# Rows of the next image asked for one piece a band, four bands ahead of their use

## The chip, the cores and the metric

The kernel runs on one core of one Trainium2 chip. The metric is device time in microseconds (us) of one execution, from the first to the last instruction of the program with what little lies around it; several executions are taken and their median is given. The engines are named as in the profile: PE is TensorE's matmul and PEld its weight load, DVE is VectorE, ACT is ScalarE, POOL is GpSimd, SP is SyncE. A "q" behind a name (SPq) is that engine's sequencer, which issues DMAs.

## What is computed

The input is 32 images of 96 channels and 56 x 56 pixels in float32. Two layers follow each other.

```python
# layer 0: inverted bottleneck with squeeze and excitation, 576 hidden channels
h = silu(bn(conv1x1(x, fake_quant(w1))))
h = silu(bn(depthwise3x3(h, fake_quant(w2))))
s = sigmoid(se_w2 @ silu(se_w1 @ mean(h, (2, 3))))
x = x + bn(conv1x1(h * s, fake_quant(w3)))
# layer 1: two attentions, then a gated mix of a plain and a deformable 3x3 convolution
mag = abs(rfft2(x))                      # first spectrum
ca = channel_attention(mag)              # one number a channel
sa = spatial_attention(mean(x), l2(x), resized(mean(mag)))   # one number a pixel
y = x * ca * sa
aux = concat(y, coordinates, resized(mean(abs(rfft2(y)))))   # second spectrum
offset, gate = conv3x3(aux), sigmoid(conv1x1(relu(conv3x3(aux))))
z = (1 - gate) * conv3x3(y) + gate * deformable_conv(y, offset)
out = relu(batch_norm_over_all_images(z) + x)
```

## The kernel before, in words

**Streams.** `layers` (from line 942) runs three pieces of work beside each other. The *bands* of image b are the main stream: an image has seven bands of eight rows (`NBD` = 7, `RB` = 8), and a band n is offsets (`offsets`, line 644), interpolation weights (`weights_load` and `weights`, lines 681 to 696), sampling (`sample_tiles`, line 716), the deformable convolution (`deform`, line 738) and the join with the plain convolution (`combine`, line 779). Beside them go `second(b + 1)`, which is `attend` (line 437): the projection that ends layer 0, the first spectrum, the channel and spatial attention, and the second spectrum of the next image; and `first(b + 2)`, which is `hidden` (line 203): the expansion and depthwise convolution of the image after that. `pump` (line 1015) advances the two side streams in proportion to the slots of the bands. Band 5 (`turn`, line 1009) of image b is where `second(b + 1)` is drained and the side streams start anew.

**Offsets are two bands ahead.** During band n the kernel runs `find(n + 2)`, which convolves the rows of the band after next (`joint_conv`, line 619). So the last two bands of image b already read the first rows of image b + 1. A convolution of band j reads rows 8j - 1 to 8j + 8; the sampling of band j reads rows 8j - 2 to 8j + 9 (`block_channels`, line 699).

**One buffer for y.** The image y = x * ca * sa lies in a single padded tile `yp` (line 956), so rows of the next image take the place of rows of this one as these fall free. `refill(b, upto)` (line 1034) brings rows of image b in, up to a row number, in pieces of at most eight rows, if the spatial attention of that image exists (`("sa", b) in p`). For each piece `load_rows` (line 581) issues two DMAs: the rows of layer 0's output from memory, on SP's queue (line 584), and the piece's spatial attention, broadcast to 96 partitions, on GpSimd's queue (line 586) into a tile `sab` of a pool with two buffers. Four slots later (line 1041) `attend_rows` multiplies the rows in place by both attentions on VectorE (line 592). `refill` also loads the rows of the second spectrum's feature, channel 100 of `yp`, once that feature exists (`load_freq`, line 596, on SP's queue).

**When rows are asked for, before.** At the end of band j the kernel asks for the next image's rows up to 8(j + 1) - 2, which is what band j has set free, and after band 6 for all 56 (line 1150). At the beginning of band 5 it asks for rows up to 38 (line 1113), and `flush` runs every postponed step at once, the multiplications among them. The pieces that result are 8, 8 and 6 rows at the end of band 2, 8 at the ends of bands 3, 4 and 5, and 8 and 2 at the end of band 6.

**What the second spectrum needs.** `dft_mag` (line 338) takes the image in six blocks of sixteen channels, three tiles `x2` in turn. For the second spectrum each block is loaded on SP's queue (line 361), multiplied by the spatial attention on GpSimd (`weigh`, line 366), transformed on TensorE (line 386) and copied by ScalarE (line 393). The sums over channels (line 427) end each spectrum and are read by TensorE at line 430.

**Order.** Each engine runs its instructions in order. The order on SP's queue is the order of the program text (line 1354). On the other engines a scheduler, which plans with its own durations, arranges the instructions, except where an order is kept by hand (`keep_in_program_order`: the depthwise activation, the offsets' `Abs` at line 673 and the weights' product at line 695).

**Other lines that are spoken of.** L168 is the expansion's matmul and L172 its activation; L261 and L259 are the depthwise taps on VectorE, L221 their activation; L284 to L296 the squeeze and excitation; L305 loads the hidden activations `hq` back for the projection at L323 and L329; L605 and L634 are the offsets' and the plain convolution; L654 copies the offsets out and L658 stores them, L670 loads them back as `ht`, L673 and L674 make them weights, stored at L677; L688 and L689 load these as `wc` and `wr`, L695 multiplies them; L706 copies blocks for the transposes at L710, L712 copies the result; L724 samples, L728 and L735 copy and pack; L743 is the deformable convolution; L766 and L757 make the gates of two bands at a time; L782 to L785 are the join; L1049 stores z.

Of the kernel before, what the change touches and what calls it, by code (L numbers as in the profile page):

```python
# [16 lines left out]
C, H, W = 96, 56, 56  # L17
# [3 lines left out]
RB = 8  # L21
# [9 lines left out]
PD = 2  # L31
# [3 lines left out]
NBD = H // RB  # L35
# [27 lines left out]
NQB = 8  # L63
KG = 3
AHEAD = 1
READY = 1
KS = 15
TAB = HP * WP
# [512 lines left out]
def load_rows(nc, p, yp, b, x1, r0, r1):  # L581

    rows = yp[:C, PD + r0 : PD + r1, PD : PD + W]
    nc.sync.dma_start(rows, x1.rearrange("c (h w) -> c h w", h=H)[:, r0:r1])
    sab = p["q2"].tile([C, RB, W], FP, name="sab")[:, : r1 - r0]
    nc.gpsimd.dma_start(sab, p["sa", b].rearrange("o (h w) -> o h w", h=H)[:, r0:r1].to_broadcast([C, r1 - r0, W]))
    return rows, sab


def attend_rows(nc, p, b, rows, sab):  # L590

    nc.vector.scalar_tensor_tensor(rows, rows, p["ca", b], sab, ALU.mult, ALU.mult)


def load_freq(nc, p, yp, b, r0, r1):
    nc.sync.dma_start(yp[CA - 1 : CA, PD + r0 : PD + r1, PD : PD + W], p["fq", b][:, r0:r1])
# [96 lines left out]
def weights(nc, p, wc, wr):  # L693

    p["tc"].keep_in_program_order(nc.vector.tensor_tensor(wc, wc, wr, ALU.mult))  # L695
    return wc


def block_channels(nc, p, yp, j, h):

    yt = p["yt"].tile([2 * NS, NTH, C], FP, name="yt")
    yb = p["ybl"].tile([C, NTH, 2, SB, SB], FP, name="ybl")
    src = yp[:C, j * RB : j * RB + SB, h * NTH * TS : h * NTH * TS + SB]
    for s in range(2):
        blocks = bass.AP(src.tensor, src.offset + s * TS * WY, [src.ap[0], [TS, NTH], [WY, SB], [1, SB]])
        nc.gpsimd.tensor_copy(yb[:, :, s], blocks)  # L706
    for lo, hi in ((0, 4), (4, NTH)):
        pt = bank(p)
        for t in range(lo, hi):
            nc.tensor.transpose(pt[:, (t - lo) * C : (t - lo + 1) * C], yb[:, t].rearrange("c s r x -> c (s r x)"),  # L710
                                p["w"]["ident"][:C, :C])
        nc.scalar.copy(yt[:, lo:hi].rearrange("p t c -> p (t c)"), pt[:, : (hi - lo) * C])  # L712
    return yt


def sample_tiles(nc, p, yt, s, v, group):


    pts = [(bank(p), bank(p)) for _ in group]
    for (lo, hi), pt in zip(group, pts):  # L720
        for t in range(lo, hi):
            for k in range(2):
                ps = slice(k * NS, (k + 1) * NS)
                nc.tensor.matmul(pt[k][:C, (t - lo) * KP : (t - lo + 1) * KP], yt[ps, t], s[ps, t * KP : (t + 1) * KP],  # L724
                                 start=True, stop=True)
    for (lo, hi), pt in zip(group, pts):
        for k in range(2):
            nc.scalar.copy(v[:C, :, lo:hi, k].rearrange("c k t p -> c t k p"),  # L728
                           pt[k][:C, : (hi - lo) * KP].rearrange("c (t k p) -> c t k p", t=hi - lo, k=NTAP))


def pack(nc, v):

    for i in range(3):
        nc.scalar.copy(v[C:, 1 + 2 * i : 3 + 2 * i], v[i * QC : (i + 1) * QC, KA:])  # L735
# [25 lines left out]
def gates_of(nc, p, hid):  # L761

    pgs = bank(p), bank(p)
    for i, pg in enumerate(pgs):
        ps = slice(i * NS, i * NS + DMID)
        nc.tensor.matmul(pg[:C, :BW], p["w"]["dg2p"][ps], hid[ps], start=True, stop=True)  # L766
    return [gate_from(nc, p, pg) for pg in pgs]
# [174 lines left out]
def layers(tc, a, dp, x1d, zd, stats, far):  # L942
# [7 lines left out]
    B = x1d.shape[0]  # L950
    with ExitStack() as ctx:
# [8 lines left out]
                                 ("ca", 2), ("s1p", 1), ("xc", 2), ("sp", 1), ("sq", 1), ("q1", 3), ("q2", 2), ("hid", 2), ("yb", 4),  # L960
                                 ("off", 1), ("st", 2), ("ht", 1), ("wc", READY + AHEAD + 1), ("wr", AHEAD + 1), ("yt", 2), ("ybl", 1),
                                 ("vp", 2)))
# [18 lines left out]
        def flush():  # L981
            while later:
                later.pop(0)[1]()
# [27 lines left out]
        def start(b, length):  # L1011
            streams[:] = [[second(b + 1), 0, n_second, slot + 3, slot + length - 8],
                          [first(b + 2), 0, n_first, slot, slot + length]]

        def pump():
            nonlocal slot
            slot += 1
            for st in streams:
                due = st[2] * min(1.0, (slot - st[3]) / (st[4] - st[3]))
                while st[1] < due:  # L1020
                    st[1] += 1
                    next(st[0], None)
            later.sort(key=lambda e: e[0])
            while later and later[0][0] <= slot:
                later.pop(0)[1]()

        def drain():
            for st in streams:
                for _ in st[0]:
                    pass  # L1030
# [3 lines left out]
        def refill(b, upto):  # L1034

            upto = min(H, upto)
            r = filled.get(("y", b), 0)
            while ("sa", b) in p and r < upto:
                r1 = min(upto, r + RB)
                args = load_rows(nc, p, yp, b, x1d[b], r, r1)  # L1040
                later.append((slot + 4, lambda args=args: attend_rows(nc, p, b, *args)))
                r = filled["y", b] = r1
            r = filled.get(("fq", b), 0)
            if ("fq", b) in p and r < upto:
                load_freq(nc, p, yp, b, r, upto)
                filled["fq", b] = upto
# [29 lines left out]
        bands = [(b, j) for b in range(B) for j in range(NBD)]  # L1076
        hids, gates, ybs, hds, ready = [], [], [], [], []

        def find(n):
            if n % 2 == 0:  # L1080
                hids.append(p["hid"].tile([2 * NS, BW], FP, name="hid"))
            hid = hids[n // 2][n % 2 * NS : n % 2 * NS + DMID]
            return offsets(nc, p, yp, bands[n][1], top[:, n % NBD : n % NBD + 1], hid, ybs, hds)
# [11 lines left out]
        def prepare(upto):  # L1095

            nonlocal n_loads
            while n_loads < min(upto, 2 * len(hds)):
                n, m = divmod(n_loads, 2)
                loads.append(weights_load(nc, p, hds[n], m))  # L1100
                n_loads += 1

        prepare(READY + AHEAD)
        for _ in range(READY):
            ready.append(weights(nc, p, *loads.pop(0)))
        yts = [block_channels(nc, p, yp, 0, 0)]
        start(0, turn * (NTX + 2))
        for n, (b, j) in enumerate(bands):
            if j == 0:
                st = p["st"].tile([C, NBD, 6], FP, name="st")  # L1110
            if j == turn:
                drain()
                refill(b + 1, j * RB - PD)
                flush()
                start(b + 1, slots)
            more = find(n + 2) if n + 2 < len(bands) else iter(())
            next(more, None)
            for h in range(2):
                v = p["vp"].tile([128, NTAP, NTH, 2, TP], FP, name="v")
                prepare(2 * n + h + READY + AHEAD)  # L1120
                s = ready.pop(0)
                yt = yts.pop(0)
                for i, group in enumerate(GROUPS):
                    sample_tiles(nc, p, yt, s, v, group)
                    for _ in range(group[0][0], group[-1][1]):
                        next(more, None)
                        pump()
                    if i == 0:
                        for end in ends:
                            end()  # L1130
                        ends.clear()
                        if h == 1 and n + 1 < len(bands):
                            yts.append(block_channels(nc, p, yp, bands[n + 1][1], 0))
                        ready.extend(weights(nc, p, *ws) for ws in loads[:1])
                        del loads[:1]
                        if h == 0:
                            yts.append(block_channels(nc, p, yp, j, 1))
                pack(nc, v)
                if h == 0:
                    if n % 2 == 0:  # L1140
                        gates.extend(gates_of(nc, p, hids[n // 2]))
                    gate = gates.pop(0)
                ends.append(lambda n=n, h=h, v=v, gate=gate, st=st: end_half(n, h, v, gate, st))
            for _ in more:
                pass
            pump()
            pump()
            pump()
            if b + 1 < B:
                refill(b + 1, (j + 1) * RB - PD if j < NBD - 1 else H)  # L1150
            if j == NBD - 1:
                nc.vector.tensor_reduce(top[:, NBD:], top, AX.X, ALU.max)
        for end in ends:
# [349 lines left out]
```

## Time and profile before

| what | value |
|---|---|
| median of three runs | 9370.22 us (9349.59 to 9405.27) |
| the profiled execution | 9376.95 us, its span 9375.2 us |
| TensorE busy, mean granted clock | 8247.2 us (88%), 0.929 |
| VectorE busy | 7137.8 us (76%) |
| ScalarE busy | 5367.0 us (57%) |
| GpSimd busy | 2663.1 us (28%) |
| row multiplications (L592) | 255 |
| row loads (L584), attention loads (L586), feature loads (L596) | 255, 255, 100 |

How to read the lines of the profile. A group line names the source line, the engine, the operation, the tiles written and read, their shapes, how often it ran, its busy time and mean duration, and the idle time of the engine just before it with what ended that idle time ("releaser"). A line of waits names an engine and the instruction that it could not start, what ended the wait, and then the total, the count and the longest. A line of a timeline has the start (us from the span's start), the duration, the engine, the instruction, "x" with a count where neighbours are merged, and in brackets the idle time before it and its releaser; "issue" means that the profile shows nothing that was waited for. A line of windows has a stretch of time, its length, the busy time of each engine with its number of instructions, then the granted clock (1.00 is full), the share of the DMA engines' time and GB/s. A float32 matmul is two passes in the profile, so seven matmuls of the program are fourteen instructions.

### The profile page before, as it was taken

What the parts mean: (1) busy time and instruction counts of PE and PEld (TensorE: products, weight loads), DVE (VectorE), ACT (ScalarE), POOL (GpSimd) and SP (SyncE); (2) the same over time, 40 slices, a digit from 0 to 9 for tenths busy, and PEclk for the clock granted to TensorE, in tenths of its full rate; (3) what the DMA queues carried; (4) which work ended last, traced back from release to release, by engine and by line L of the source; (5) the groups of instructions that cost most, each with busy time, mean ns of one, the idle gap of its engine ahead of it and who ended that gap; (6) DMA issues with size and microseconds to landing.
All of it is one profiled execution on the core that took longest, in us unless ns stands there. A gap on an engine that the chain in (4) does not pass through costs nothing. (4 is left out here: it accounts for less than half of the span.)

```text
span 9375.2 us, 138185 instructions
## 1 busy us (share of the span) xinstructions
PE 8247.2 (88%) x52406; PEld 5235.2 (56%) x52406; DVE 7137.8 (76%) x6724; ACT 5367.0 (57%) x10486; POOL 2663.1 (28%) x2642
## 2 busy tenths in 40 slices
PE   6889999999998999899999999999999999999870
PEld 3455555565555555555555555555555555555550
DVE  7687778888777888877788888778888877887333
ACT  2355555666655566656566655556665565665453
POOL 0123233333323332332333333233223323333210
PEclk9889999999999999999999999999999999999885
DMA  2345555555555555555555555555555555555559
GB/s 89 100 138 155 156 162 158 162 149 147 156 160 158 160 162 146 145 158 158 160 159 156 151 148 161 159 160 157 156 151 148 163 161 159 160 157 140 128 172 417
DMA packets 1069507, 1486.53 MB, mean 159 GB/s; under 512 B 590438, under 2 KB 840086, under 8 KB 1056550
## 3 DMA queue, kind: packets, MB, share of 16 engines
q1 hardware_dynamic: 858747, 985.20, 38.6%
q10 hardware_dynamic: 153803, 329.80, 9.5%
q0 software_dynamic: 56288, 162.60, 6.9%
q8 instruction: 421, 6.90, 0.3%
q14 instruction: 248, 2.03, 0.1%
HBM read 1064.29 MB, written 412.65 MB: 158 GB/s over the span
## 5 line engine op out<-in xcount | busy, mean ns | idle before, releaser
L261 DVE SCALAR_TENSOR_TENSOR acch<-hp,w,acch 128x1512 f32<-128x1512 f32 (+1 forms) x2250 | 4316.7, 1919 | 35.5
L743 PE MATMUL pd<-v,c_def 128*96 128x224 f32 (+1 forms) x6272 | 1489.9, 387 | 242.9 <-ACT v L735 210.3
L605 PE MATMUL mm<-yp,c_jointW 104*128 104x448 f32 x4032 | 1671.2, 566 | 2.3 <-DMA yp<-fqd 1.8
L706 POOL COPY ybl<-yp 96x448 f32<-96x448 f32 x896 | 1131.3, 1289 | 1643.6 <-PE mm L710 1641.8
L743 PEld LDWEIGHTS pd<-v,c_def 128*96 128x96 f32 (+1 forms) x6272 | 1074.9, 178 | 553.8 <-ACT v L735 244.5
L605 PEld LDWEIGHTS mm<-yp,c_jointW 104*128 104x128 f32 x4032 | 774.6, 196 | 773.0 <-issue 730.1
L168 PE MATMUL mm<-xt,w 96*128 96x392 f32 (+3 forms) x2688 | 1060.1, 529 | 34.1 <-DMA xt<-in_x 33.1
L724 PE MATMUL mm<-wc,yt 64*96 64x144 f32 x12544 | 1049.0, 296 | 30.2 <-ACT hp L172 13.2
L172 ACT ACTIVATE hp<-mm,sh,inv 128x392 f32<-128x392 f32 (+2 forms) x1216 | 813.1, 673 | 442.7 <-PE mm L168 390.4
L728 ACT COPY v<-mm 96x288 f32<-96x288 f32 (+1 forms) x2688 | 1002.1, 444 | 101.9 <-PE mm L724 68.2
L695 DVE TENSOR_TENSOR wc<-wc,wr 128x1008 f32<-128x1008 f32 x448 | 575.9, 1286 | 609.7 <-DMA wr<-hd 594.5
L724 PEld LDWEIGHTS mm<-wc,yt 64*96 64x96 f32 x12544 | 824.8, 161 | 324.1 <-issue 167.7
L323 PE MATMUL mm<-hq,w3s 128*96 128x392 f32 x2048 | 798.2, 536 | 158.0 <-DMA hq<-h2d 156.6
L634 PE MATMUL mm<-yp,c_base0W 96*64 96x224 f32 x8064 | 828.1, 357 | 0.0
L658 POOL DMA_DIRECT2D od<-at x224 | 186.3, 832 | 2168.2 <-DVE at L654 1466.3
L735 ACT COPY v<-v 32x448 f32<-32x448 f32 x1344 | 755.2, 562 | 29.8
L634 PEld LDWEIGHTS mm<-yp,c_base0W 96*64 96x64 f32 x8064 | 553.5, 135 | 276.0 <-issue 69.5
L712 ACT COPY yt<-mm 128x384 f32<-128x384 f32 (+1 forms) x896 | 349.8, 439 | 509.1 <-PE mm L710 499.6
L221 ACT ACTIVATE acch<-acch,sh,inv 128x1568 f32<-128x1568 f32 x288 | 488.6, 1697 | 261.3 <-DVE acch L261 259.0
L323 PEld LDWEIGHTS mm<-hq,w3s 128*96 128x96 f32 x2048 | 339.6, 174 | 512.6 <-issue 315.7
L386 PE MATMUL mm<-c_FU,x 112*128 112x116 f32 x3072 | 464.3, 299 | 181.3 <-POOL x L366 160.7
L625 ACT ACTIVATE hid<-mm,c_dg1b 50x448 f32<-50x448 f32 x224 | 140.7, 628 | 814.8 <-PE mm L605 803.3
(194 smaller groups left out, 9060.3 us busy)
## 6 DMA issues: line engine op xcount, KB each, us to landing
h2d<-acch ACTq DMA_DIRECT2D x288, 784.0 KB
wc<-hd SPq DMA_DIRECT2D x896, 252.0 KB
wr<-hd SPq DMA_DIRECT2D x896, 252.0 KB
hq<-h2d SPq DMA_DIRECT2D x128, 980.0 KB
hq<-h2d SPq DMA_DIRECT2D x128, 784.0 KB
x<-x1d SPq DMA_DIRECT2D x768, 98.0 KB
ht<-od SPq DMA_DIRECT2D x224, 252.0 KB
hd<-ht ACTq DMA_DIRECT2D x224, 252.0 KB
```

The source lines that it names most:

```text
L168: nc.tensor.matmul(pt[p0 : p0 + w1.shape[1], : rows * W], w1, xts[hf][:, r0 * W : (r0 + rows) * W], start=True, stop=True)
L172: nc.scalar.activation(h1[lo:hi, row0 : row0 + rows, 1 : 1 + W], pt[lo:hi, : rows * W].rearrange("p (h w) -> p h w", h=rows), AF.Silu, bia ...
L261: nc.vector.scalar_tensor_tensor(acc[:, lo:hi], win, wk, acc[:, lo:hi], ALU.mult, ALU.add)
L323: nc.tensor.matmul(pts[half][:C, :EW], w3s[:, ch], hq, start=(i == 0), stop=False)
L605: nc.tensor.matmul(view, weights[:, k], yp[:channels, r0 : r0 + RB, dx + PD - 1 : dx + PD - 1 + W], start=(k == 0), stop=(k == NTAP - 1))
L634: nc.tensor.matmul(pb[i * BC : (i + 1) * BC, : BW // 2].rearrange("p (h w) -> p h w", h=RB // 2), w["base"][:, k], yp[:C, r0 + i * RB // 2 ...
L695: p["tc"].keep_in_program_order(nc.vector.tensor_tensor(wc, wc, wr, ALU.mult))
L706: nc.gpsimd.tensor_copy(yb[:, :, s], blocks)
L724: nc.tensor.matmul(pt[k][:C, (t - lo) * KP : (t - lo + 1) * KP], yt[ps, t], s[ps, t * KP : (t + 1) * KP], start=True, stop=True)
L728: nc.scalar.copy(v[:C, :, lo:hi, k].rearrange("c k t p -> c t k p"), pt[k][:C, : (hi - lo) * KP].rearrange("c (t k p) -> c t k p", t=hi - ...
L735: nc.scalar.copy(v[C:, 1 + 2 * i : 3 + 2 * i], v[i * QC : (i + 1) * QC, KA:])
L743: nc.tensor.matmul(out.rearrange("c q (t x) -> c t q x", x=TS), p["w"]["def"][ks, k], v[ks, k].rearrange("c t s (r x) -> c t (s r) x", r=T ...
```

## The change

The next image's rows are asked for by the band that will need them. At the end of band n the kernel looks up the band four further on, number jn of image bn, and asks for the rows of bn up to 8(jn + 2). Band jn's offsets are convolved in band n + 2 and need rows up to 8jn + 8. At the beginning of band 5 it asks for rows up to 24 instead of 38. For images whose attention is there by then, the pieces are two of eight rows at the end of band 3, and one of eight rows at the ends of bands 4, 5, 6 and, of the next image's own bands, 0 and 1. An image has seven pieces of eight rows instead of six of eight, one of six and one of two, and the feature rows come in five loads (24, 8, 8, 8, 8) instead of three (38, 8, 10).

```diff
 AHEAD = 1
+NEXT = 4
 READY = 1
...
             if j == turn:
                 drain()
-                refill(b + 1, j * RB - PD)
+                refill(b + 1, 3 * RB)
                 flush()
                 start(b + 1, slots)
...
-            if b + 1 < B:
-                refill(b + 1, (j + 1) * RB - PD if j < NBD - 1 else H)
+            if n + NEXT < len(bands):
+                bn, jn = bands[n + NEXT]
+                refill(bn, (jn + 2) * RB)
```

## The prediction

> **What bounds the kernel now.** I read the page's busy row first:
>
> ```profile
> PE 8247.2 (88%) x52406; PEld 5235.2 (56%) x52406; DVE 7137.8 (76%) x6724; ACT 5367.0 (57%) x10486; POOL 2663.1 (28%) x2642
> ```
>
> TensorE sets the pace, so a change is worth what it does to TensorE's idle time. The table of waits names that time and, two lines of it, VectorE and GpSimd stopping at the rows that the change moves:
>
> ```profile
> POOL sab L586 <- DVE yp L592: 694.5, 158, 13.5
> ...
> PE mm L386 <- POOL x L366: 160.7, 38, 7.9
> ...
> DVE yp L592 <- issue: 120.8, 29, 6.0
> ...
> PE acc L430 <- DVE m_fe L427: 61.0, 31, 2.6
> ```
>
> (us in total, times, longest.) Whether these belong together only one image's timeline can say. I took the image that passes through 4000 to 4280 us. GpSimd:
>
> ```profile
> 4189.56 6.63 POOL L366 TENSOR_TENSOR x<-x,sa 112x448 f32<-112x448 f32 x3
> 4196.15 1.06 POOL L586 DMA_DIRECT2D sab<-sad  x2
> ...
> 4200.84 0.52 POOL L586 DMA_DIRECT2D sab<-sad  x1 [2.80 <-DVE yp L592]
> ...
> 4203.05 3.44 POOL L706 COPY ybl<-yp 96x448 f32<-96x448 f32 x2
> ...
> 4207.68 2.57 POOL L366 TENSOR_TENSOR x<-x,sa 112x448 f32<-112x448 f32 x1
> ```
>
> VectorE:
>
> ```profile
> 4199.86 0.68 DVE L592 SCALAR_TENSOR_TENSOR yp<-yp,ca,sab 96x448 f32<-96x448 f32 x1 [4.14 <-issue]
> 4201.56 0.68 DVE L592 SCALAR_TENSOR_TENSOR yp<-yp,ca,sab 96x448 f32<-96x448 f32 x1 [1.02 <-DMA sab<-sad]
> ```
>
> TensorE:
>
> ```profile
> 4198.36 0.74 PE L710 MATMUL mm<-c_ident,ybl 96*128 96x96 f32 x7
> ...
> 4204.49 0.93 PE L168 MATMUL mm<-xt,w 96*128 96x392 f32 x2
> 4210.30 2.06 PE L386 MATMUL mm<-c_FU,x 112*128 112x116 f32 x8 [4.89 <-POOL x L366]
> 4212.15 5.21 PE L743 MATMUL pd<-v,c_def 96*96 96x224 f32 x14
> ```
>
> The reader sees a chain. VectorE comes to the first piece of next rows before its attention map `sab` (asked for at 4196.15) has landed and stands 4.14 + 1.02 us. GpSimd's third map needs the buffer of the first, so GpSimd stands 2.80 us behind VectorE, and again before the fourth and fifth. Its copies for the transposes and its fourth weighed block of the second spectrum queue behind these. TensorE lacks that block for 4.89 us, and then works at half clock: L743's fourteen matmuls take 5.21 us, against 2.82 us for an equal group at 4195.71.
>
> Two neighbouring images, by windows, are an experiment within the trace:
>
> ```profile
> 5371.00:5647.00 276.00, 252.22 (x1629) 160.14 (x1629) 220.98 (x199) 164.87 (x326) 81.81 (x82) 0.94 0.56 155
> 5647.00:5917.00 270.00, 250.75 (x1622) 159.35 (x1623) 220.69 (x199) 163.90 (x324) 85.87 (x82) 0.96 0.58 159
> ```
>
> (us, busy of PE, PEld, DVE, ACT, POOL, granted clock, DMA share, GB/s.) The wait at L386 is 6.5 us in the first and 3.5 us in the second. The images differ by 6 us, twice that, at equal work.
>
> **The change part by part.** *Where rows are asked for.* Before, `second` has its attention map by the end of band 2, and the refill there takes three pieces (8, 8 and 6 rows) at once. After, the first refill that names the next image is at the end of band 3: two pieces, then one at the ends of bands 4, 5, 6, 0 and 1. In the changed program's order VectorE has no L592 between L665 and the next sums of the depthwise taps, where two stood; its first two come about thirty microseconds of work later. GpSimd's order is the three weighed blocks, one map, the offsets' store, one map, the copies, the fourth block. Two maps need no buffer that is still in use.
>
> *TensorE's gain there.* GpSimd would end its three blocks at 4196.2, two maps and the store (0.52 + 0.85 + 0.52) at 4198.1; the copies need L710, done at 4199.1, and with their crowded 3.44 us end at 4202.5; the fourth block, 2.57 us, at 4205.1. TensorE asks at 4205.4. The fifth block stands behind a store of `z`; VectorE's new order (three taps 5.5, L782 0.68, two taps with L783 and L784 4.8 us) gives that `z` at 4206.7, the block at 4209.5, and TensorE asks at 4211. So the wait goes: 146.9 us over 28 images in the groups from 1000 to 8700 us, 5.2 us an image. Half clock behind it cost 2.4 us at L743 and 1.0 us at L386 in this image (5.21 less 2.82, 2.06 less 1.05); in the two others L743 took 4.30 and 4.50 us, so about 2.65 as a mean. Together 7.85.
>
> *VectorE's gain.* The chain goes on through VectorE to the second spectrum's sum (m_fy), which TensorE awaits at L430. VectorE loses stalls of 5.2, 6.4 and 3.8 us in the three images, 5.1 as a mean, and has two multiplications there instead of four, 1.36 us against 0.68 x 3 + 0.85 = 2.89. That is 6.6 us, less than TensorE's 7.85. I take 6.6: past this point TensorE would wait on VectorE. The ends are 5.2 (no clock regained) and 9.4, which is the pair's slope of 1.9 on a mean gap of 5.
>
> *Clock.* The windows show 0.50 granted from 4210.3 to 4216.9 behind the 4.89 us gap, and also from 4145.4 to 4152.0 behind a gap of 2.00 us. The Trainium skill, "TensorE: Matmul & The Clock Gate", Part 1, ties the half rate to at least one idle window of about 3.4 us; by it the 2.00 us gap should cost nothing and the shorter L386 gaps of 3.5 us little, so TensorE's gain would be an estimated 6.5 us (5.2 and half of 2.65) instead of 7.85, and the sum below 168 instead of 171 us. The trace disagrees on the 2.00 us gap, and the measurement decides.
>
> *Pieces six and seven* now stand in bands 0 and 1, ahead of the first spectrum's sum (m_fe), whose wait of 2.00 us at L430 is already uncovered. On SP's queue each adds a row load (0.5 us) and a one-row frequency load (0.65 us) ahead of the next weights; an image has 12 such issues instead of 11. The weights that follow have cover: in that band the product L695 ran at 4397.5, its first reader on TensorE at 4409.9. VectorE reaches the seventh piece about when its rows land behind the `ht` load (issued 4405.2). No row shows this. Below: 0 or a small gain, as VectorE idles 1.31 and 2.05 us at the L414s just there. Above: 6.0, the longest stall of any L592. All nine waits for row loads sum to 55.5 us, so the near row is small; I take 0.6 us an image.
>
> *Band 6* loses a two-row piece (0.33 us of VectorE) and *the turn* keeps one piece and its forced multiplication; the frequency load there still waits for its store (SP 373.0 us in 32 waits), as before. In the changed order three of L743's seven taps stand behind the turn's offset convolution, which TensorE so reaches 1.2 us sooner (6/14 of 2.82). Its last input is the frequency row: from 0 to 1.2 us; waits of L605 on it come to 1.8 us in all, so I take 0.3. `pd` is then ready later, and VectorE's join with it, but VectorE idles 190.8 us in 32 waits at L292 right behind: hidden. Were that idle gone, 0.7 us a multiplication would show.
>
> *GpSimd* issues 31 maps fewer at 0.52 us, and each later map waits for a multiplication that now stands before the offsets' copy in VectorE's order, for which GpSimd's next store waits anyway: nothing. *Bytes* stay, 56 rows an image.
>
> *Sum.* The early short images have other gaps, so 30 images count: 30 x (-6.6 + 0.6 + 0.3) = -171 us. The profiled execution took 9376.95 us (span 9375.2), 6.7 above the median 9370.22 and inside the three runs. 9370 - 171 = 9199; I say 9200. With the ends for every term: 30 x (-9.4) gives 9090, 30 x (-5.2 + 0.6 + 1.2) gives 9268.
>
> **The rivals.** *Half comes back on GpSimd.* The copy pair ran 2.32 us at 4176.83 and 3.44 over busy VectorE; with VectorE no longer standing, copies and blocks may take longer than the 0.3 us margin allows. Three such operations each held one tap (1.85 us) make the block 5 us late at worst; half of the 6.6 returned leaves 30 x (3.3 - 0.9) = 72, so 9298. For it: the small margin. Against: in the second of the pair L766 and L757 fill in and give a margin over 1 us. The Trainium skill, "SBUF — State Buffer", Who interferes with whom, says that a VectorE instruction with two SBUF inputs and a GpSimd one that reads SBUF exclude each other, the later one waiting to the end. The longer copies agree.
>
> *TensorE's time passes to the next wait.* If weights, `hq` loads (143.1 us over 28 images) or `ht` set the period by themselves, nothing moves: 9370. Against: those gaps keep their distance to the image's start in long and short images (5 to 6 us each in both of the pair).
>
> *Slower.* The seventh piece stalls VectorE ahead of m_fe. Each microsecond adds one to L430's wait, and the clock's share with it. With 2.65 more of half clock it decides from 6.6 - 0.3 - 2.65 = 3.65 us, and at 6.0 an image gets 2.35 us longer, 30 images 70: 9440. For it: a row load shares its queue with eight weight loads. Against: in SP's order it precedes that band's weights, and the earlier eight were issued by 4390.9.
>
> *The change does nothing*: excluded in the order, where the pieces move.
>
> **How the numbers follow.** Forecast 0.65, half back 0.12, next wait 0.11, slower 0.12. 0.5% is about 47 us, what a measurement of this kernel can tell from no change. Faster by more: 0.65 + 0.12 = 0.77; within: 0.11; slower: 0.12. The forecast's own range is 9090 to 9270. Leaving out the slower case, the upper part of the unchanged one and the last 20 us of the extreme gain, the range is 9110 to 9345.
>
> **What the profile after would show.** L386's wait on L366 near zero (right) or still over 2 us an image (half back); no L592 idle by "issue"; the sab wait on GpSimd shorter; L743 behind it back at 2.8 us; images of 267 to 269 us. L430's wait for m_fe above 4 us, or L592 waiting for row loads by 100 us and more, would make me wrong, and so would a longer `hq` or `ht` wait that takes up the time.

## The result and the profile after

The changed kernel takes 9241.88 us (median of four runs, 9237.53 to 9255.58), beside 9368.36 us for the kernel before on the same chip (four runs). The ratio is 0.9863, with a 95% interval from 0.9831 to 0.9895: it is faster by 1.4%, 126 us. The forecast was 9200 us, 171 us less than before, so three quarters of the gain came. The profiled execution took 9239.07 us, its span 9237.3 us.

In the changed kernel's profile a line number is one higher than before from L67 on, and two higher from the refill at a band's end on. The text goes on with the numbers of before; the profile's lines have their own.

The page's busy row, then some lines of the table of waits (us in total, times, longest):

```profile
PE 8221.8 (89%) x52406; PEld 5208.4 (56%) x52406; DVE 7198.1 (78%) x6693; ACT 5369.4 (58%) x10486; POOL 2529.9 (27%) x2611
```

```profile
POOL sab L587 <- DVE yp L593: 1043.8, 128, 15.4
...
DVE yp L593 <- DMA yp<-x1d: 81.8, 29, 11.4
```

The multiplications no longer stop VectorE by "issue"; that row is gone. GpSimd waits longer for them than before (1043.8 against 694.5 us), not less. The timeline of one image shows why that costs nothing. GpSimd:

```profile
4397.36 6.63 POOL L367 TENSOR_TENSOR x<-x,sa 112x448 f32<-112x448 f32 x3
4403.95 1.05 POOL L587 DMA_DIRECT2D sab<-sad  x2
4404.99 0.85 POOL L659 DMA_DIRECT2D od<-at  x1
4407.43 2.56 POOL L707 COPY ybl<-yp 96x448 f32<-96x448 f32 x2 [1.59 <-PE mm L711]
4410.35 2.62 POOL L367 TENSOR_TENSOR x<-x,sa 112x448 f32<-112x448 f32 x1 [0.36 <-DMA x<-x1d]
...
4435.80 1.10 POOL L587 DMA_DIRECT2D sab<-sad  x2 [15.16 <-DVE yp L593]
```

Two maps pass without a wait, and the 15.16 us come after all six blocks are done. TensorE, in the same stretch:

```profile
4413.02 1.15 PE L387 MATMUL mm<-c_FU,x 112*128 112x116 f32 x8 [0.19 <-POOL x L367]
4414.01 2.81 PE L744 MATMUL pd<-v,c_def 96*96 96x224 f32 x14
```

The wait of 4.89 us is 0.19 us here, and the fourteen matmuls behind it run at full clock, 2.81 us where they took 5.21. Over 28 images (708 to 8255 us; before, 708 to 8381) TensorE's waits in the changed kernel are:

```profile
PE pd L744 <- ACT v L736: 189.4, 66, 8.0
PE mm L324 <- DMA hq<-h2d: 140.4, 28, 6.3
PE acc L431 <- DVE m_fe L428: 54.6, 27, 2.2
PE mm L725 <- ACT hp L173: 36.1, 40, 1.5
...
PE mm L606 <- ACT sq L414: 17.4, 22, 2.1
PE mm L387 <- POOL x L367: 8.0, 15, 2.4
...
PE mm L606 <- DMA yp<-fqd: 7.3, 5, 1.9
```

The wait at the transform fell from 146.5 to 8.0 us; two lower lines are new or longer. The same 28 images, worked out from the trace's records as means of an image (idle time of TensorE by the line that it then went on with; half clock is the time at 0.50):

| us an image | before | after |
|---|---|---|
| period | 274.01 | 269.54 |
| TensorE idle | 22.04 | 18.19 |
| of it ahead of L386 (transform) | 5.23 | 0.31 |
| L743 (deformable convolution) | 8.13 | 7.44 |
| L724 (sampling) | 0.43 | 1.41 |
| L605 (offsets' convolution) | 0.03 | 0.89 |
| TensorE busy | 251.97 | 251.35 |
| busy in L743 and L386 | 57.17 | 54.93 |
| half clock | 28.77 | 25.72 |

So 4.92 us of waiting and 2.24 us of half clock behind it went, as the chain in the prediction says, and 1.84 us came back as waits at L724 and L605, with half clock behind them (a granted clock of 0.50 in the stretch after the gap). 28 images times 4.47 is 125 of the 138 us between the two profiled executions (9376.95 and 9239.07 us); by the medians the gain is 126 us.

### The profile page after: what moved, and what is told of

The parts are those of the page before. It is cut to its first block, busy times and chain, and to the rows that moved or that the text cites. A ratio compares the mean times of both kernels' runs of the same rounds, so it can differ in the third digit from the quotient of the medians.

```text
span 9237.3 us, 138081 instructions
## 1 busy us (share of the span) xinstructions
PE 8221.8 (89%) x52406; PEld 5208.4 (56%) x52406; DVE 7198.1 (78%) x6693; ACT 5369.4 (58%) x10486; POOL 2529.9 (27%) x2611
## 3 DMA queue, kind: packets, MB, share of 16 engines
q14 instruction: 249, 2.04, 0.1%
## 5 line engine op out<-in xcount | busy, mean ns | idle before, releaser
L262 DVE SCALAR_TENSOR_TENSOR acch<-hp,w,acch 128x1512 f32<-128x1512 f32 (+1 forms) x2250 | 4397.3, 1954 | 38.2
L744 PE MATMUL pd<-v,c_def 128*96 128x224 f32 (+1 forms) x6272 | 1450.9, 378 | 225.2 <-ACT v L736 201.6
L707 POOL COPY ybl<-yp 96x448 f32<-96x448 f32 x896 | 1079.8, 1232 | 1698.5 <-PE mm L711 1697.5
L744 PEld LDWEIGHTS pd<-v,c_def 128*96 128x96 f32 (+1 forms) x6272 | 1046.2, 174 | 524.7 <-ACT v L736 229.2
L467 POOL TENSOR_TENSOR o<-o,xc 96x392 f32<-96x392 f32 x256 | 366.3, 1431 | 679.3 <-ACT o L334 677.8
```

The source lines that it names most:

```text
L262: nc.vector.scalar_tensor_tensor(acc[:, lo:hi], win, wk, acc[:, lo:hi], ALU.mult, ALU.add)
L744: nc.tensor.matmul(out.rearrange("c q (t x) -> c t q x", x=TS), p["w"]["def"][ks, k], v[ks, k].rearrange("c t s (r x) -> c t (s r) x", r=T ...
```

## The experiments

The reading that was tested is that the gain comes from the order of maps and multiplications around band 3. In the expectations this is the theory called Order; its rivals put the gain on SP's queue (Queue) or on there being one piece a band instead of three (Spread). Later groups name their theories themselves. Every time is a median beside runs of the kernel before on the same chip, and the ratio is to these. Two edited kernels often ran on different chips, on which the kernel before took 9368 to 9383 us, so a difference between two of them is good to some 15 us.

**Nothing asked at band 2.**

```diff
-            if b + 1 < B:
+            if b + 1 < B and j > 2:
```

> The kernel before with one thing changed: the end of band 2 asks for no rows. Everything later is asked for as before (30 rows at the end of band 3 in four pieces, 8 and 2 rows at the end of band 6). Order theory (the gain comes from the first multiplications and attention maps no longer standing ahead of the second spectrum's fourth block): nearly all of the gain, 9240 to 9275 us, TensorE's wait for L366 under 1 us an image. Spread theory (it comes from seven equal pieces, two of them in bands 0 and 1): 9340 to 9370. Queue theory (it comes from the three row loads that stood on SP's queue ahead of weights at the end of band 2): 9240 to 9275 as well.

Measured: 9344.85 us, ratio 0.9957 (0.994 to 0.9975). By its wait at the block this is Order, by its time Spread (9340 to 9370 us), and it misses the 9240 to 9275 us of Order and Queue. The three pieces of band 2 are now asked for with the one of band 3, and four multiplications stand among the squares (L414) of the second spectrum. TensorE's waits over 28 images:

```profile
PE mm L724 <- ACT yb L639: 56.8, 24, 2.8
...
PE mm L724 <- ACT hp L172: 35.7, 26, 1.5
PE mm L605 <- ACT sq L413: 22.2, 23, 2.3
...
PE mm L386 <- POOL x L366: 7.0, 13, 2.4
```

The wait for the block is gone as in the changed kernel (7.0 us), and yet only 33 us are won: the idle time ahead of L724 is 3.45 us an image, 2.04 more than in the changed kernel, whose period is 3.78 us shorter. Taking the pieces away from band 2 removes the wait; that two and not four land among the squares is about half of the rest. This last is read from the trace and was not tried by itself. Spread holds its part.

**The kernel before, multiplications kept in program order five slots later; the changed kernel with them in program order.**

```diff
-    nc.vector.scalar_tensor_tensor(rows, rows, p["ca", b], sab, ALU.mult, ALU.mult)
+    p["tc"].keep_in_program_order(nc.vector.scalar_tensor_tensor(rows, rows, p["ca", b], sab, ALU.mult, ALU.mult))
...
-                later.append((slot + 4, lambda args=args: attend_rows(nc, p, b, *args)))
+                later.append((slot + 9, lambda args=args: attend_rows(nc, p, b, *args)))
```

> The kernel before with the rows asked for exactly where they were, but every row multiplication kept in program order and placed nine slots after its load instead of four. In the program's order the first three multiplications now stand behind L783 and L784 of that band, and the third map behind the fourth weighed block. Order theory: VectorE's stalls of 4 and 1 us go and the fourth block comes in time, 9235 to 9275 us, TensorE's wait for L366 under 1 us an image. Queue theory: the loads stand on SP's queue as before, so 9350 to 9375. Spread theory: 9350 to 9375.

Measured (both edits, in the kernel before): 9324.81 us, ratio 0.9942 (0.9925 to 0.9959), 50 us above what Order expected and 25 us below Queue and Spread. VectorE passes the first two pieces without a stop, but three maps are still asked for there, and the stop moves to the third. GpSimd, VectorE and TensorE in one image:

```profile
4188.83 0.76 POOL L586 DMA_DIRECT2D sab<-sad  x1 [4.53 <-DVE yp L592]
```

```profile
4187.96 0.57 DVE L592 SCALAR_TENSOR_TENSOR yp<-yp,ca,sab 96x336 f32<-96x336 f32 x1 [4.66 <-issue]
```

```profile
4190.80 2.06 PE L386 MATMUL mm<-c_FU,x 112*128 112x116 f32 x8 [4.50 <-POOL x L366]
```

The chain is the same one with a later piece and, this time, the sixth block. By this trace it hangs on the number of maps asked for there against two buffers, not on one place in VectorE's order; a third buffer for `sab` was not tried.

> The changed kernel with the row multiplications kept in program order, four slots after their loads. The first two then stand behind the second spectrum's sum instead of among its squares (L414). If VectorE at those squares is what TensorE waits for now (L605 for the squares' copies 17 us and L724 for L172 36 us over 28 images, 12 in the kernel before), these waits fall to the old ones and an image gains 1 to 2 us: 9185 to 9220 us. If the squares are not the limit, 9235 to 9250; the third and fourth map then wait for later multiplications ahead of the store of the feature row, and L605's wait for that row may grow.

Measured (the first edit alone, in the changed kernel): 9367.15 us, ratio 0.9996 (0.9987 to 1.0006): the whole gain was lost, which neither theory expected. The wait for the block stays away (0.88 us an image ahead of L386), but the wait ahead of L743 at about 100 us into an image grew from 6.0 to 9.3 us. In band 0 VectorE's multiplication of the fifth piece now runs beside the projection's outputs, where GpSimd's addition takes 4.27 us, and the map that waited for it (that of the seventh piece) stands between their stores:

```profile
4345.98 4.27 POOL L467 TENSOR_TENSOR o<-o,xc 96x392 f32<-96x392 f32 x1 [1.24 <-ACT o L334]
...
4352.72 0.52 POOL L587 DMA_DIRECT2D sab<-sad  x1
4353.23 0.51 POOL L468 DMA_DIRECT2D x1d<-o  x1
```

In the changed kernel the same addition takes 2.26 us as a mean (here 4.24) and no map stands between the stores. SP's six loads of the first spectrum wait for these stores, and the offsets' load `ht` is behind them on the queue. That this chain is the cause is read from the trace; it was not tried by itself.

**Rows asked for five bands ahead.**

```diff
-NEXT = 4
+NEXT = 5
```

> The changed kernel with the look ahead of five bands instead of four: two pieces at the end of band 2, then one a band. In the program's order two multiplications stand right behind L665 again and four maps ahead of the copies for the fourth block. Order theory: VectorE stands about 5 us and TensorE waits 3 us and more an image for L366, 9310 to 9375 us. Queue theory: two row loads instead of three ahead of the weights, a third of the loss, 9270 to 9300. Spread theory: seven equal pieces in bands 2 to 0, close to the changed kernel, 9235 to 9270.

Measured: 9360.87 us, ratio 0.9983 (0.9973 to 0.9993), as expected by Order. The multiplications are back where they stood before the change, with the same stop:

```profile
4184.98 1.28 DVE L593 SCALAR_TENSOR_TENSOR yp<-yp,ca,sab 96x448 f32<-96x448 f32 x2 [5.83 <-issue]
```

```profile
4185.97 1.10 POOL L587 DMA_DIRECT2D sab<-sad  x2 [4.50 <-DVE yp L593]
```

The idle time ahead of L386 is 3.72 us an image. Still one piece a band later on and the same loads on SP's queue, one band earlier, and nearly nine tenths of the gain are gone: Queue (9270 to 9300 us here) falls, and Spread alone (9235 to 9270 us) falls with it.

**VectorE's time and GpSimd's time, each by itself.** Two edits of the changed kernel add work to one engine and leave the order of the others.

```diff
     nc.sync.dma_start(ht.rearrange("q n k -> q (n k)"), src)
+    for _ in range(9 if j == 5 else 0):
+        p["tc"].keep_in_program_order(
+            nc.vector.tensor_reduce(top, at.rearrange("o t s p -> o (t s p)"), AX.X, ALU.max, apply_absolute_value=True))
```

> The changed kernel with nothing but VectorE work added: in each image nine repeats of the 0.53 us maximum (L666, same result), five right behind the join and four among the next taps, 4.8 us in all, ahead of the squares of the second spectrum. No other engine's order moves, GpSimd's blocks are not touched. Theory Path (as in the prediction: VectorE's own time carries the chain on to the second spectrum's sum, and 6.6 us of VectorE was what could be won): an image gets 4 to 5 us longer, 9360 to 9395 us, with waits at the sampling and at the sum of the second spectrum up by as much. Rival Cover (VectorE has slack there, only GpSimd's fourth block held TensorE): 9235 to 9265 us. In between, the difference from 9242 divided by 30 x 4.8 is the share of VectorE's time that counts.

Measured: 9326.94 us, ratio 0.9947 (0.9928 to 0.9965), between the two theories. 85 us more than the changed kernel is 2.8 us an image (2.41 by the periods of the two profiled executions) for 4.8 us of added work. But VectorE was busy for only 2.3 us an image more (225.17 instead of 222.85 us): in the changed kernel one depthwise tap in each image takes 4 to 5 us, and here no tap takes more than 2.72 us (the section after this one shows the long tap). What VectorE lost on balance passed to TensorE about one to one, which is the reading of Path. It shows at the sampling, not at the sum of the second spectrum:

```profile
PE mm L728 <- ACT yb L640: 47.1, 24, 2.8
PE mm L728 <- ACT hp L173: 38.1, 40, 1.5
...
PE acc L431 <- DVE m_fy L428: 8.0, 23, 0.9
```

```diff
         if gate is not None and g < NG:
+            for _ in range(4 if g == 3 else 0):
+                nc.gpsimd.tensor_copy(x2s[g][:, :, :W], x2s[g][:, :, :W])
```

> The changed kernel with nothing but GpSimd work added: in each image four copies of the fourth block of the second spectrum onto itself (same result), 1.05 us each alone and up to 1.9 beside VectorE, 4.2 to 7.6 us, just ahead of its weighing. VectorE's order is not touched. Theory Both (as in the prediction: TensorE's wait for the block costs its length and the half clock behind it, whatever VectorE does): the wait of TensorE at the transform for GpSimd comes back with 3 to 6 us an image, image 4 to 7 us longer, 9360 to 9450 us. Rival VectorE alone (the period was set by VectorE, a late block is made up later): wait back, but image under 1.5 us longer, 9242 to 9285 us.

Measured: 9451.23 us, ratio 1.0087 (1.0058 to 1.0115), slower than the kernel before and 1 us above the range of Both. The four copies took 6.7 us an image. TensorE's waits over 28 images:

```profile
PE mm L389 <- POOL x L369: 187.5, 27, 9.0
```

That is 6.7 us an image, and the image took 7.0 us more (209 us over 30), although the waits at L724, L605 and L430 fell by 2.7 us at the same time; the one at L743 rose by 1.7 us and half clock from 25.72 to 31.94 us. A late block costs TensorE its length, with half clock behind it, while VectorE's busy time stays at 222.8 us an image.

**Where the two multiplications stand.**

```diff
-    nc.vector.scalar_tensor_tensor(rows, rows, p["ca", b], sab, ALU.mult, ALU.mult)
+    mul = nc.vector.scalar_tensor_tensor(rows, rows, p["ca", b], sab, ALU.mult, ALU.mult)
+    if r < 2 * RB:
+        p["tc"].keep_in_program_order(mul)
...
```

> The changed kernel with the first two pieces' multiplications kept in program order, which puts them behind the second spectrum's sum instead of among its squares; all other pieces stand as before. Theory Squares (the new waits of the changed kernel, at the sampling and the offsets' convolution, 1.8 us an image more than before the change, come from two multiplications standing among the squares): these waits go, 1.8 to 2.5 us an image, 9167 to 9195 us. Rival (the waits have another cause, or the multiplications hold the join behind the sum instead): 9230 to 9260 us.

Measured: 9252.16 us, ratio 0.9874 (0.9849 to 0.9899): the rival. The wait at the sampling fell as Squares says (ahead of L724 from 1.41 to 0.53 us an image), and the deformable convolution 240 to 260 us into the image took it up (from 1.45 to 2.9 us). The wait of the offsets' convolution did not fall but rose, from 0.89 to 1.58 us: for the squares it is 20.5 us in 28 images (17.4 in the changed kernel), and for the frequency row 23.6 (7.3). TensorE and ScalarE at the deformable convolution:

```profile
4191.51 1.11 PE L746 MATMUL pd<-v,c_def 128*96 128x224 f32 x4 [2.67 <-ACT v L738]
```

```profile
4190.10 0.78 ACT L676 ACTIVATE ht<-ht,c_blk 112x576 f32<-112x576 f32 x1 [1.92 <-DMA ht<-od]
4190.90 0.56 ACT L738 COPY v<-v 32x448 f32<-32x448 f32 x1
```

ScalarE stands for the offsets' load `ht`, and the packing copies queue behind. By this trace the next limit is that load.

```diff
-                later.append((slot + 4, lambda args=args: attend_rows(nc, p, b, *args)))
+                if r >= 2 * RB:
+                    later.append((slot + 4, lambda args=args: attend_rows(nc, p, b, *args)))
```

> The changed kernel without the multiplications of the first two pieces of each image (rows 0 to 15 stay without both attentions; their loads and maps are still issued), so that 1.3 us of VectorE is gone from among the second spectrum's squares and put nowhere else. Theory Work (these two multiplications are what the new waits at the sampling and the offsets' convolution pay for, wherever they stand): 1.3 to 2 us an image less, 9180 to 9205 us. Rival Next (the load of the offsets, ht, sets the following half band, as it did when the multiplications were put behind the sum): the waits at the sampling fall and the wait of the deformable convolution for the packing grows by as much, 9225 to 9255 us.

Measured: 32019.26 us, which says nothing on the theories: without the attention the offsets left the reach of the sampling's blocks, and the kernel ran its general branch (`gather_block`) after the main part. The main part can still be compared with that of the changed kernel by its period: 270.44 us an image against 269.54. The idle time ahead of L724 fell from 1.41 to 0.36 us, the one ahead of L743 240 to 260 us into the image rose from 1.45 to 2.5 us, and the one ahead of L386 rose from 0.31 to 1.77 us. GpSimd's timeline shows why: with no multiplication to wait for, the third and fourth map moved ahead of the fourth block, and such maps wait for the landing of an earlier one (110.2 us, 48 times in 28 images). So the edit also brought back part of the old wait. The period does not fall, as in the run before it, but by itself this run does not tell the two theories apart.

**The two pieces in bands 0 and 1.**

```diff
-                refill(bn, (jn + 2) * RB)
+                refill(bn, H if j == NBD - 1 else (jn + 2) * RB)
```

> The changed kernel with the last three pieces all asked for at the end of band 6, as the kernel before does with its last two, so that none is asked for in bands 0 and 1 of the next image. The prediction charged the two pieces in bands 0 and 1 with 0.6 us an image. Theory Free (they cost nothing, their loads and multiplications stand in VectorE's and SP's spare time): 9235 to 9265 us, the wait for the first spectrum's sum unchanged at 2.0 us an image; the three maps in a row may cost a little by GpSimd. Rival Charged (two row loads and two feature loads ahead of the weights cost 0.6 us or more): 9200 to 9225 us.

Measured: 9237.7 us, ratio 0.9853 (0.983 to 0.9877), the same as the changed kernel: Free. In the changed kernel the pieces cost nothing there.

**The next limit, and both kernels without it.** The same one step in either kernel:

```diff
-    for _ in range(4):
+    for _ in range(3):
         yield
     ht = p["ht"].tile([SB * NTX, 4, KP], FP, name="ht")
```

> The same earlier ht load in the kernel before the change. If the two waits (for GpSimd's block in band 3, for ht in band 0) are separate terms, this gains about as much here as in the changed kernel, and the change is worth 120 to 135 us with it as without it. If one wait takes the place of the other, the gains of the two edits do not add: the pair together is then worth less than their sum by 30 us or more.

> The changed kernel with the offsets' load ht issued one step of the band earlier, which on SP's queue puts it ahead of the six loads of the next image's first spectrum in band 0, and ahead of the four weight loads in bands 4 and 5. TensorE's longest wait of the changed kernel is there: 5 to 6 us an image, 98 us into it, the deformable convolution waiting for the packing behind ht. Theory Queue (the load stands behind six loads that wait for stores of layer 0's output): this wait falls below 1.5 us, images 4 to 6 us shorter, 9060 to 9125 us. Rival Next (another load or VectorE's chain to the first spectrum's sum takes it up): 9200 to 9245 us. Slower if the weight loads that now stand behind ht come late: above 9260 us.

Measured: in the kernel before 9258.06 us, ratio 0.9881 (0.9864 to 0.9897), a gain of 111 us; in the changed kernel 9322.66 us, ratio 0.9951 (0.9934 to 0.9967), a loss of 81 us against 9241.88. That is the range of Slower, though the weights that it had in mind are not what TensorE waits for. So the gains do not add: 126 and 111 us apart, 47 us together. The wait ahead of L743 fell in both (to 2.96 and 2.23 us an image, from 8.13 and 7.44). In the changed kernel TensorE's idle time fell even below its former 18.19 us, to 17.28, and still the image took 3.3 us longer, since TensorE was busy for 255.57 instead of 251.35 us: half clock rose from 25.72 to 32.18 us. A new wait at the first spectrum's transform (L386 behind the squares of L372: 51.4 us in 28 images) is in the other kernel too (47.0 us) and does not part the two. Only the changed kernel has new waits of about 2 us 138 to 146 us into each image, about the end of band 1:

```profile
PE mm L169 <- ACT yt L713: 49.8, 28, 2.0
```

The timeline of VectorE there, and the waits for row loads between 900 and 8400 us, first of this kernel and then of the changed one:

```profile
4114.31 0.68 DVE L593 SCALAR_TENSOR_TENSOR yp<-yp,ca,sab 96x448 f32<-96x448 f32 x1 [3.00 <-DMA zd<-z]
```

```profile
DVE yp L593 <- DMA yp<-x1d: 96.0, 26, 6.1
```

```profile
DVE yp L593 <- DMA yp<-x1d: 19.2, 19, 3.2
```

This is the seventh piece. (The line names a store of `z`, which landed 0.04 us after the row load; 26 other such waits are put down to the row load.) Its row load was issued at 4103.76, so it was used 10.5 us later; in the changed kernel an equal one, issued at 4334.46, was used at 4341.48 after a wait of 0.26 us. In the 28 images the load took 9.2 to 11.8 us from its issue to its landing, in the changed kernel at most 7.5 us where VectorE waited for it. Two squares of the first spectrum stand behind it, ScalarE's next square behind these (2.32 us), and ScalarE's copies for TensorE behind that.

**Both edits together**: the `ht` step of the last diff and the `H if j == NBD - 1` of the one before it, in the changed kernel.

> The changed kernel with both edits that were tried apart: ht's load one step earlier, and the last three pieces asked for at the end of band 6, none in bands 0 and 1. With the earlier ht alone the seventh piece's multiplication waited 3.0 us for its row load ahead of two of the first spectrum's squares, and TensorE stood 2.3 us an image more at 130 to 150 us into it, and ran at half clock behind that (half clock 32.2 us an image against 25.7). Theory Piece (this wait, the one that the prediction named as the way to a slower kernel, is what turned ht's gain of 111 us in the kernel before into a loss of 81 us in the changed one): it goes, with 2 to 4 us of half clock, 9130 to 9195 us, faster than either kernel. Rival Loads (the first spectrum's loads and the sampling hold what ht gives up): 9250 to 9320 us.

Measured: 9206.57 us (9193.01 to 9215.76), ratio 0.9816 (0.98 to 0.9831), faster than either kernel, 12 us above what Piece expected and 43 us below Loads. Half clock is back at 25.11 us an image, the idle time ahead of L168 and L710 fell from 2.33 to 0.12 us or less, and VectorE no longer waits for row loads in that stretch. What is left is elsewhere:

```profile
PE mm L324 <- DMA hq<-h2d: 137.8, 28, 7.4
PE acc L431 <- DVE m_fe L428: 55.4, 28, 2.0
PE pd L744 <- ACT v L736: 48.9, 70, 1.7
PE mm L725 <- ACT hp L173: 42.3, 36, 1.5
```

So the pieces in bands 0 and 1, which cost nothing in the changed kernel, cost 116 us (9322.66 less 9206.57; 126 by the ratios) once `ht` is loaded earlier. Even without them the two gains do not add fully: 177 us here, 126 and 111 apart.

## Why the prediction was right, and where it was off

*TensorE's wait at L386* (5.2 us): right. 4.92 us of it went, along the chain of map, multiplication, GpSimd and block that was named; five bands ahead brings the chain back, and an added delay of the block alone costs 7.0 us an image. The upper end of the forecast had taken two neighbouring images for an experiment, 6 us for 3 us of this wait; the 4.92 us that went were worth 4.47.

*Half clock behind it* (2.65 us): right in place, L743 and L386 are busy 2.24 us less. But the new gaps at L724 and L605 have half clock of their own: L724, L766, L605, L410 and L168 are busy 1.4 us more, so that TensorE's busy time fell by 0.62 us only.

*VectorE's 6.6 us, taken as the smaller of two*: this is the term that was mis-sized. The period fell by 4.47 us, which with the other two terms as they came (0 and 0.23) leaves 4.7 for it. The stops did go: 116.8 us by "issue" and 28.9 us behind `sab` in 28 images, 5.2 us an image against 5.1. The 1.5 us of the two multiplications did not. From the spatial attention (L276) to the second spectrum's sum (L427) VectorE takes 57.8 us an image before and 52.5 after, 5.3 less, and all of that is idle time: its own work there is 48.7 and 48.6 us. What the multiplications freed was taken up by one depthwise tap, which got longer. VectorE and GpSimd at GpSimd's last two blocks, in the kernel before and in the changed one:

```profile
4213.84 4.19 POOL L366 TENSOR_TENSOR x<-x,sa 112x448 f32<-112x448 f32 x2
4217.07 8.62 DVE L261 SCALAR_TENSOR_TENSOR acch<-hp,w,acch 128x1568 f32<-128x1568 f32 x4
4218.08 4.08 POOL L706 COPY ybl<-yp 96x448 f32<-96x448 f32 x2
```

```profile
4417.32 10.62 DVE L262 SCALAR_TENSOR_TENSOR acch<-hp,w,acch 128x1568 f32<-128x1568 f32 x4
4417.41 2.23 POOL L367 TENSOR_TENSOR x<-x,sa 112x448 f32<-112x448 f32 x2
4419.59 1.05 POOL L707 COPY ybl<-yp 96x448 f32<-96x448 f32 x2
```

GpSimd's two blocks and two copies take 8.5 us as a mean before and 3.6 after. The first of the four taps beside them takes 5.0 us in the changed kernel (4 to 5 us in each of the 28 images); the longest tap before takes 2.72. The rival "half comes back on GpSimd" named this collision, but expected it to lengthen GpSimd's work and not VectorE's. That the one holds up the other is read from these lines; no run was made for it, though the tap is short again in the run with nine maxima, where these stand beside the same GpSimd work.

The second thing is the places that the two multiplications moved to, which were costed at nothing: among the squares they hold ScalarE, which shares one tile of squares with VectorE (its wait for that tile rose from 74.4 to 105.0 us in 28 images), and through it the sampling. The sampling's 0.98 us an image fell again by 0.88 when they were put behind the sum and by 1.05 when they were left out. The 0.86 us at the offsets' convolution (0.23 of it the turn's, below) did not, and the cause of the rest stays open. The walk along the changed order had stopped at "about thirty microseconds of work later". Even so, moving the multiplications away gave nothing back, since the deformable convolution then waits for the offsets' load. So the term was also limited by the next wait, which the prediction had only as a rival for the whole gain.

*Pieces six and seven* (0.6 us): the wait for m_fe did not move (55.7 before, 54.6 us after, 28 images), and the run without them measured the same time; the term was zero. By luck it hid part of the shortfall of the term above. The slower rival built on the seventh piece did not decide (L592 waits for row loads by 81.8 us in all, under the 100 us that were named as a sign), but its mechanism is real: one edit later it stalled VectorE by 96.0 us in 26 waits.

*The turn* (0.3 us): L605's wait for the frequency row rose from 0.8 to 7.3 us in 28 images, 0.23 us an image. Right.

*GpSimd's maps* at nothing: right in the sum. That its wait behind multiplications would be shorter was wrong, it is longer, and nothing waits for it.

*Half back on GpSimd*: did not come in this form; the block is rarely late (15 times, 2.4 us at most). What came of it stands above.

*Images of 267 to 269 us*: 269.54 as a mean, just above. The time stayed inside its range (9110 to 9345 us) and moved the way that was forecast.

## What to carry to other kernels

A wait that goes is worth at most the distance to the next one on the same stretch, so forecast a gain by walking the changed order up to the next thing that the engine needs, and cost the place to which work is moved as carefully as the place that it leaves. An engine that no longer stands still may run beside another one that it did not meet before, so do not take its instructions at their old lengths. A piece of work that costs nothing where its data lands just in time is a debt: the next edit that shifts a queue may call it in, so try improvements together and not only one by one. Where idle time falls and the kernel's time does not, look at the granted clock: many short gaps can cost more than one long one.

## What the runs showed of the hardware

Half clock lasts a whole number of steps: in the kernel before, every one of the 133 spells of half clock between 700 and 8300 us lasted 3.41 us (47), twice that (72) or three times that (14). Of single gaps of TensorE (no other above 0.3 us within 16 us), in the two kernels together none of the 42 below 1 us was followed by half clock, 42 of the 56 between 1.5 and 2.5 us were, and so were all 139 above 3 us. The Trainium skill, "TensorE: Matmul & The Clock Gate", Part 1, gives the same window of about 3.4 us and ties the half rate to one that is idle; the lengths of the spells agree, and the gaps of 1.5 to 2.5 us do not, being shorter than a window. The sum by that rule (168 us) and the one by the trace (171 us) lie too close for the result, 126 us, to tell them apart. The term itself does: 2.24 us an image went at L743 and L386, nearer to the 2.65 us of the trace than to half of it.
